# Attention heads told apart by row groups instead of masked copies, with the maximum as a ninth row of the score matmul

## The chip, the cores and the metric

The kernel runs on one core of one Trainium2 chip. The metric is the device time of one execution in microseconds (us), the median of several runs. The core has a matrix engine (TensorE: PE for matmuls, PEld for its weight loads), VectorE (DVE), ScalarE (ACT), GpSimd (POOL) and SyncE (SP), which here issues most DMAs. "Granted clock" is the share of TensorE's full clock that the throttle lets through.

## The reference, cut to what matters

One decoder layer with pre-norm: self attention, cross attention to a context, and a mixture of experts. `x` is 64 batches of 128 tokens with 128 features, the context 64 batches of 77 tokens, all in float32. There are 16 heads of 8 features, so that each head's score matmul contracts over only 8 rows.

```python
def _L0_xattn_ref(query, key, value, mask, Wq, bq, Wk, bk, Wv, bv, Wo, bo):
    q = _split_heads(query @ Wq.T + bq)          # 16 heads of 8
    k = _split_heads(key @ Wk.T + bk)
    v = _split_heads(value @ Wv.T + bv)
    scores = jnp.einsum('bhqd,bhkd->bhqk', q, k) / np.sqrt(D_K)
    scores = jnp.where(mask[:, None, :, :] == 0, -1e9, scores)
    p_attn = jax.nn.softmax(scores, axis=-1)
    attn = jnp.einsum('bhqk,bhkd->bhqd', p_attn, v)
    x = attn.transpose(0, 2, 1, 3).reshape(B, S, D_MODEL)
    return x @ Wo.T + bo

x = x + self_attention(layernorm(x))             # no mask, q scaled by 1/sqrt(128), no bias on q, k, v
x = x + cross_attention(layernorm(x), ctx, mask)
x = x + experts(layernorm(x))                    # router, top 2 of 8, 128 -> 512 -> 128
```

## The kernel before

The 64 batches are held in 16 groups of four (`GB`). Attention is a list of 32 jobs: the 16 groups of self attention, then the 16 of cross attention. A job has four units, one for each batch. Sixteen heads are four groups `c` of four heads (`NG`, `HG`), and group `c` is rows 32c to 32c+31 of the transposed queries and keys. One matmul serves four heads at once: one operand has a masked copy for each head, in which the rows of the three other heads are zero.

- `prologue` prepares a job in five items: `norm` (POOL: xn, L159, and the residual's bias row, L166), `trans` (PE transposes, ACT copies xnT), `query` (pq, L236, to qT on DVE, L239 or L241), `key` (pk, L246, to kT on ACT; then POOL writes four masked copies km, L258, and four of the scaled queries qm, L262) and `value` (pv, L271).
- `maxima` computes a unit's scores with queries as rows (`ps`, L292). In cross attention DVE overwrites masked places (`copy_predicated`, L299). DVE takes the negated maximum over the keys (L304).
- `split` cuts the maxima of two units into three bfloat16 parts on POOL. `turn` transposes them on PE (`pm`, L327), ACT copies them (`mt`), and SP sends them to DRAM (`md`, L331) and back as three rows for each `c` (`mrow`, L335).
- `masked` (L350) starts the transposed score tile `pt` of cross attention with a bias matmul; `scores` (L362) adds keys times masked queries; `exps` adds the three rows of the maximum (L374), and ACT takes the exponential (L380).
- `values` (L394) multiplies the exponentials with the values and with ones, four head groups side by side as column groups. DVE divides (reciprocal, L401). `project` (L414) applies the output weights, DVE adds the residual (L418) and takes the statistics for the next norm; `root` computes the reciprocal roots on POOL by a power and a Newton step (L148 to L153).

The order on PE is written out by hand (`manual_schedule`); the other engines' orders come from a scheduler that follows the dependencies. The main loop goes over steps `s`: unit `s` has its maxima taken, unit `s-4` its exponentials, unit `s-5` its values. A step has two half-steps. In a half-step, two score tiles of the one unit and two transposed ones of the other are interleaved on PE, one in each of the four row groups; then come the values, and then one item of a list `todo` that holds the next job's prologue, the turns and the projections. The pools `ps_s`, `ps_t`, `ps_o` and `ps_m` have two PSUM buffers each. In steady state a job's eight half-steps end with, in order: pm, pv, tp, py, pm, pq, pk, py.

Before the loop, the statistics and roots of all 16 groups are computed, and the first job's prologue runs alone. After the attention come the router and the experts (L478 on), which the change leaves alone.

Of the kernel before, what the change touches and what calls it, by code (L numbers as in the profile page):

```python
# [8 lines left out]
F32 = mybir.dt.float32  # L9
I32 = mybir.dt.int32  # L10
# [6 lines left out]
H = 16  # L17
# [10 lines left out]
def decoder_layer(  # L28
# [33 lines left out]
    def load(src, shape, name, eng=None):  # L62
# [27 lines left out]
    neg_s = const.tile([P, HG, S2], F32, tag="neg_s", name="neg_s")  # L90
    nc.gpsimd.memset(neg_s, NEG)


    blk = const.tile([P, H], F32, tag="blk", name="blk")
    nc.gpsimd.memset(blk, 1.0)
    nc.gpsimd.affine_select(
        out=blk, in_=blk, compare_op=ALU.is_ge, fill=0.0, base=0,
        pattern=[[-DH, H]], channel_multiplier=1,
    )
    nc.gpsimd.affine_select(  # L100
        out=blk, in_=blk, compare_op=ALU.is_ge, fill=0.0, base=DH - 1,
        pattern=[[DH, H]], channel_multiplier=-1,
    )
    hm = const.tile([P, HG], F32, tag="hm", name="hm")
    nc.vector.tensor_reduce(hm, blk.rearrange("p (g j) -> p j g", j=HG), AX.X, ALU.add)

# [7 lines left out]

    vms = []
    for n in range(3):
        t = const.tile([P, GB * NG, HG, 32 + DH], F32, tag=f"vm{n}", name=f"vm{n}")
        nc.gpsimd.memset(t, 0.0)
        vms.append(t)

# [3 lines left out]
    ones_b = const.tile([P, P], BF16, tag="ones_b", name="ones_b")  # L124
    nc.gpsimd.memset(ones_b, 1.0)
# [60 lines left out]

    def attention():
        jobs = [(cross, g) for cross in (False, True) for g in range(NGRP)]
        NB = len(jobs) * GB
        with (  # L190
            tc.tile_pool(name="grp", bufs=2) as grp,
# [6 lines left out]
        ):  # L198
            G = [dict() for _ in jobs]
# [11 lines left out]
            def prologue(n):  # L211
# [6 lines left out]
                def norm():  # L218
                    loads(n + 1)
                    v["xn"] = normalised(g)  # L220
                    add_row(g, bo_s if cross else bff_s)
                    if cross:
                        v["off"] = grp.tile([P, GB, S2], I32, tag="off", name="off")
                        nc.vector.tensor_scalar(v["off"], v["mask"], 0.0, None, ALU.is_equal)
                        v["bias"] = grp.tile([P, GB, S2], BF16, tag="bias", name="bias", bufs=3)
                        nc.gpsimd.tensor_scalar(
                            v["bias"], v["mask"], 0.0, NEG, ALU.is_equal, ALU.mult
                        )
# [4 lines left out]

                def query():
                    pq = ps_m.tile([P, T], F32, tag="mm", name="pq")
                    nc.tensor.matmul(pq, wq_, v["xnT"], start=True, stop=True)  # L236
                    v["qT"] = grp.tile([P, T], F32, tag="qT", name="qT")
                    if cross:
                        nc.vector.tensor_scalar(v["qT"], pq, bq_s, scale, ALU.add, ALU.mult)  # L239
                    else:  # L240
                        nc.vector.tensor_scalar(v["qT"], pq, scale, None, ALU.mult)  # L241

                def key():
                    src = v["ctx"].rearrange("p b k -> p (b k)") if cross else v["xnT"]
                    pk = ps_m.tile([P, GB, K], F32, tag="mm", name="pk")
                    nc.tensor.matmul(  # L246
                        pk.rearrange("p b k -> p (b k)"), wk_, src, start=True, stop=True
                    )
                    v["kT"] = grp.tile([P, GB, K], F32, tag="kT", name="kT", bufs=3)
                    if cross:  # L250
                        nc.scalar.activation(v["kT"], pk, AF.Identity, bias=bk_s)
                    else:
                        nc.scalar.copy(v["kT"], pk)

                    v["km"] = grp.tile([P, GB, HG, K], F32, tag="km", name="km")
                    v["qm"] = grp.tile([P, GB, HG, S], F32, tag="qm", name="qm", bufs=3)
                    for j in range(HG):
                        nc.gpsimd.tensor_scalar(  # L258
                            v["km"][:, :, j, :], v["kT"], hm[:, j : j + 1], None, ALU.mult
                        )  # L260
                    for j in range(HG):
                        nc.gpsimd.tensor_scalar(  # L262
                            v["qm"][:, :, j, :], v["qT"].rearrange("p (b t) -> p b t", t=S),
                            hm[:, j : j + 1], None, ALU.mult,
                        )
# [18 lines left out]

            def maxima(i, c):
                n, b = divmod(i, GB)
                cross = jobs[n][0]
                v = G[n]
                K = S2 if cross else S
                rows = slice(32 * c, 32 * c + 32)  # L290
                ps = ps_s.tile([P, HG, K], F32, tag="s", name="ps")
                nc.tensor.matmul(  # L292
                    ps.rearrange("p j k -> p (j k)"),
                    v["qT"][rows, b * S : (b + 1) * S],
                    v["km"][rows, b].rearrange("p j k -> p (j k)"),
                    start=True, stop=True,
                )
                if cross:
                    nc.vector.copy_predicated(  # L299
                        ps, v["off"][:, b, :].unsqueeze(1).to_broadcast([P, HG, K]), neg_s  # L300
                    )
                if b % 2 == 0 and c == 0:
                    v["m", b // 2] = unit.tile([P, NG, 2, HG], F32, tag="m", name="m", bufs=3)
                nc.vector.tensor_reduce(  # L304
                    v["m", b // 2][:, c, b % 2, :], ps, AX.X, ALU.max, negate=True
                )

            def split(n, p):

                v = G[n]  # L310
                m = v.pop(("m", p)).rearrange("p c b j -> p c (b j)")
                mb = unit.tile([P, NG, 3, 2 * HG], BF16, tag="mb", name="mb", bufs=3)
                r = unit.tile([P, NG, 2 * HG], F32, tag="mr", name="mr", bufs=3)
                nc.gpsimd.tensor_copy(mb[:, :, 0, :], m)
                nc.gpsimd.tensor_tensor(r, m, mb[:, :, 0, :], ALU.subtract)
                nc.gpsimd.tensor_copy(mb[:, :, 1, :], r)
                nc.gpsimd.tensor_tensor(r, r, mb[:, :, 1, :], ALU.subtract)
                nc.gpsimd.tensor_copy(mb[:, :, 2, :], r)
                v["mb", p] = mb

            def turn(n, p):

                v = G[n]
                mb = v.pop(("mb", p))
                R = NG * 3 * 2 * HG
                pm = ps_m.tile([P, P], BF16, tag="mm", name="pm")
                nc.tensor.transpose(pm[:R], mb.rearrange("p c s x -> p (c s x)"), ident_b)  # L327
                mt = unit.tile([P, P], BF16, tag="mt", name="mt", bufs=3)
                nc.scalar.copy(mt[:R], pm[:R])
                md = dram.tile([R, P], BF16, tag="md", name="md")  # L330
                nc.sync.dma_start(md, mt[:R])  # L331
                mrow = unit.tile([P, 2, HG * P], BF16, tag="mrow", name="mrow", bufs=3)
                part = 2 * HG
                for c in range(NG):
                    nc.sync.dma_start(  # L335
                        mrow[32 * c : 32 * c + 3].rearrange("p b x -> p (b x)"),
# [339 lines left out]
```

## Time and profile before

| | |
|---|---|
| median of 3 runs | 2305.23 us (2303.49 to 2306.25) |
| profiled execution, its own time | 2304.34 us |
| its span, first to last instruction | 2302.6 us |
| mean granted TensorE clock | 0.884 |
| PE busy | 1971.4 us, 86% |
| PEld busy | 1250.6 us, 54% |
| DVE busy | 832.6 us, 36% |
| ACT busy | 724.5 us, 31% |
| POOL busy | 769.4 us, 33% |
| first score matmul | at 95.75 us |
| first cross attention scores | at 651.20 us |
| router and experts | from about 1294 us to the end |

How to read the lines that follow: a group of instructions has its line, engine, operation, output and inputs with their shapes and count, then the busy time in us and the mean duration in ns, then the idle time of the engine ahead of it and what ended most of that. A line of the timeline has its start in us, its length in us, engine, line and operation, and in brackets the idle time before it with what released it. A line of the list of waits has the total in us, the number of times and the longest. A row "PE" or "POOL" of digits is the span in 40 slices, in tenths busy, and "PEclk" the granted clock in tenths. A matmul in float32 is recorded as two instructions, each with a weight load.

### The profile page before, as it was taken

The numbers are of one execution on the slowest core, as the hardware profiler recorded it, in microseconds if no ns is written. First come the engines' busy times: TensorE is split into PE (matmuls) and PEld (weight loads), VectorE is DVE, ScalarE is ACT, GpSimd is POOL, SyncE is SP. The second block draws the span as 40 slices with busy tenths as digits, with TensorE's granted clock in tenths as the row PEclk, the third lists the DMA queues.
The fourth block names the chain that finished last, engine by engine and source line by source line (L and its number), as shares of the span: only waits on it lengthen the run. The fifth ranks groups of instructions, "written<-read, shape, count | busy, mean of one in ns | idle before, by whom it ended". The sixth has DMA issues, their size and how long they took to land.

```text
span 2302.6 us, 40698 instructions
## 1 busy us (share of the span) xinstructions
PE 1971.4 (86%) x17475; PEld 1250.6 (54%) x17475; DVE 832.6 (36%) x2045; ACT 724.5 (31%) x1321; POOL 769.4 (33%) x1125
## 2 busy tenths in 40 slices
PE   1297877878778788887878989999999999999999
PEld 0043433434444444444444667777777777777776
DVE  3154544545455556565656221111111111111111
ACT  0032322323222222222222343333333333333333
POOL 5955556456564646464553440000000000000000
PEclk9587878878787878787878769999999999999999
DMA  6000000000000000000000000000000000000000
GB/s 178 0 6 4 5 4 4 5 4 4 4 9 12 12 12 10 15 9 15 9 7 4 2 1 3 4 4 5 5 5 5 6 5 5 5 5 6 5 5 10
DMA packets 39940, 24.25 MB, mean 11 GB/s; under 512 B 17856, under 2 KB 37968, under 8 KB 39760
## 3 DMA queue, kind: packets, MB, share of 16 engines
q1 hardware_dynamic: 36352, 16.59, 2.8%
q0 software_dynamic: 1056, 4.19, 0.6%
q8 instruction: 136, 2.23, 0.4%
q10 hardware_dynamic: 2352, 0.88, 0.2%
q14 instruction: 44, 0.36, 0.1%
HBM read 15.89 MB, written 5.77 MB: 9 GB/s over the span
## 4 chain that ended last, share of the span: by engine, by line
PE 64%; POOL 28%; DVE 3%; issue 3%; DMA 1%; ACT 0%; SPq 0%; ACTq 0%; POOLq 0%; DVEq 0%
PE py L592 20%; PE ph L570 19%; POOL qm L262 9%; POOL km L258 7%; PE ps L292 7%; PE po L394 7%; POOL xn L159 5%; PE pt L362 2%; PE pv L271 2%; POOL xs L166 2%; PE pt L374 2%; POOL rstd L149 1%; PE pt L350 1%; PE tp L173 1%; DVE r L401 1%
## 5 line engine op out<-in xcount | busy, mean ns | idle before, releaser
L574 ACT ACTIVATE hT<-ph,b_s 128x512 f32<-128x512 f32 x512 | 351.6, 687 | 565.3 <-PE ph L570 565.3
L292 PE MATMUL ps<-km,qT 32*128 32x512 f32 (+1 forms) x1024 | 310.8, 675 | 240.5 <-POOL km L258 237.8
L592 PEld LDWEIGHTS py<-w_s,hT 128*128 128x128 f32 x4096 | 477.3, 192 | 55.7 <-issue 53.6
L380 ACT ACTIVATE e<-pt 128x512 f32<-128x512 f32 (+1 forms) x512 | 276.9, 592 | 723.1 <-PE pt L374 712.3
L592 PE MATMUL py<-w_s,hT 128*128 128x128 f32 x4096 | 481.8, 275 | 0.0
L570 PE MATMUL ph<-xT,w_s 128*128 128x512 f32 x1024 | 465.0, 597 | 1.1 <-ACT junk L508 1.1
L304 DVE TENSOR_REDUCE m<-ps 128x4 f32<-128x512 f32 (+1 forms) x512 | 286.7, 579 | 306.1 <-PE pt L362 188.0
L598 DVE SCALAR_TENSOR_TENSOR xs<-py,comb,xs 128x128 f32<-128x128 f32 x512 | 144.1, 344 | 694.5 <-PE py L592 694.5
L362 PE MATMUL pt<-qm,kT 32*128 32x512 f32 (+1 forms) x1024 | 350.6, 754 | 0.0
L570 PEld LDWEIGHTS ph<-xT,w_s 128*128 128x128 f32 x1024 | 186.4, 192 | 187.5 <-issue 186.1
L292 PEld LDWEIGHTS ps<-km,qT 32*128 32x128 f32 x1024 | 99.4, 220 | 345.5 <-POOL km L258 248.1
L159 POOL TENSOR_SCALAR xn<-xs,stat,rstd 128x128 f32<-128x128 f32 x192 | 150.6, 798 | 384.8 <-PE tp L173 384.8
L262 POOL TENSOR_SCALAR qm<-qT,hm 128x512 f32<-128x512 f32 x128 | 202.1, 1594 | 75.2 <-DVE qT L239 42.2
L299 DVE COPY_PREDICATED ps<-off,neg_s 128x308 f32<-128x308 int32 x256 | 127.6, 508 | 229.2 <-PE ps L292 226.9
L394 PEld LDWEIGHTS po<-e,vm 128*32 128x32 f32 (+1 forms) x4096 | 121.4, 123 | 103.2 <-issue 100.1
L394 PEld LDWEIGHTS po<-e,ones_w 128*32 128x32 f32 (+1 forms) x4096 | 116.2, 119 | 97.2 <-issue 95.2
L258 POOL TENSOR_SCALAR km<-kT,hm 128x512 f32<-128x512 f32 (+1 forms) x128 | 165.6, 1315 | 1.1
L394 PE MATMUL po<-e,vm 128*32 128x128 f32 (+1 forms) x4096 | 164.3, 310 | 0.0
L394 PE MATMUL po<-e,ones_w 128*32 128x128 f32 (+1 forms) x4096 | 155.5, 298 | 0.0
L401 DVE RECIPROCAL r<-po 128x256 f32<-128x256 f32 x64 | 112.3, 1755 | 37.3 <-PE po L394 37.2
L374 PE MATMUL pt<-mrow,ones_b 3*128 3x512 bf16 (+1 forms) x512 | 118.0, 430 | 0.0
L350 PE MATMUL pt<-ident_b,bias 128*77 128x512 bf16 x256 | 87.3, 426 | 0.0
(121 smaller groups left out, 1260.1 us busy)
## 6 DMA issues: line engine op xcount, KB each, us to landing
xs<-in_x_dram SPq DMA_DIRECT2D x16, 256.0 KB
w_s<-in_w_dram POOLq DMA_DIRECT2D x2, 2048.0 KB, 17.6
mrow<-md SPq DMA_DIRECT2D x256, 6.0 KB
out_dram<-xs SPq DMA_DIRECT2D x16, 256.0 KB
ctx<-in_ctxT_dram SPq DMA_DIRECT2D x16, 154.0 KB
mask<-in_mask_dram SPq DMA_DIRECT2D x16, 154.0 KB
md<-mt SPq DMA_DIRECT2D x64, 24.0 KB
wq_s<-in_wqT_dram ACTq DMA_DIRECT2D x1, 64.0 KB
```

The costliest lines, as they stand in the source:

```text
L159: nc.gpsimd.tensor_scalar(xn[:, b, :], xs[g][:, b, :], stat[:, i, 0:1], rstd[:, i : i + 1], ALU.subtract, ALU.mult,)
L258: nc.gpsimd.tensor_scalar(v["km"][:, :, j, :], v["kT"], hm[:, j : j + 1], None, ALU.mult)
L262: nc.gpsimd.tensor_scalar(v["qm"][:, :, j, :], v["qT"].rearrange("p (b t) -> p b t", t=S), hm[:, j : j + 1], None, ALU.mult,)
L292: nc.tensor.matmul(ps.rearrange("p j k -> p (j k)"), v["qT"][rows, b * S : (b + 1) * S], v["km"][rows, b].rearrange("p j k -> p (j k)"), s ...
L304: nc.vector.tensor_reduce(v["m", b // 2][:, c, b % 2, :], ps, AX.X, ALU.max, negate=True)
L362: nc.tensor.matmul(v["pt", b, c][:K].rearrange("p j q -> p (j q)"), v["kT"][rows, b, :], v["qm"][rows, b].rearrange("p j q -> p (j q)"), s ...
L374: nc.tensor.matmul(pt[:K].rearrange("p j q -> p (j q)"), ones_b[three, :K], v["mrow", b // 2][three, b % 2, :], start=False, stop=True,)
L380: nc.scalar.activation(e[:K], pt[:K], AF.Exp)
L394: nc.tensor.matmul(po[32 * c : 32 * c + 32, :], w[:, 32 * j : 32 * j + 32], v["e", b, c][:K, j, :], start=(j == 0), stop=(j == HG - 1),)
L570: nc.tensor.matmul(ph, w1_s[:, e, c * P : (c + 1) * P], xT[g], start=True, stop=True)
L574: nc.scalar.activation(hT[:, c, :], ph, AF.Gelu, bias=b1_s[:, i : i + 1])
L592: nc.tensor.matmul(py[:, b, :], hT[:, c, b * S : (b + 1) * S], w2_s[:, e * NFC + c, :], start=(c == 0), stop=(c == NFC - 1),)
```

## The change

Queries and keys get a layout in which each head has its own rows: head r of group c lies in rows 32c to 32c+7, with r along the free dimension (`qh` and `kh`, three of each, rotating over the jobs). `spread` makes it: the projected tile is written to DRAM from ACT's queue and read back by four DMAs on SP's queue, one for each c. A ninth row of `kh` is set to one once; the ninth row of `qh` receives the negated maxima, again by a trip through DRAM. A head's score matmul then contracts over 8 rows, and the transposed one over 9, which adds the maximum without a matmul of its own. The masked copies, the three-way split and the rows of the maximum go; in cross attention the mask's bias is also added to `ps` by a matmul, in place of DVE's overwriting. The scaled queries come from ACT and no longer from DVE. All four score tiles of a half-step are issued by one function.

```diff
-    neg_s = ...                                   # and blk, hm, ones_b
+    bqs_s = const.tile([P, 1], F32, tag="bqs_s", name="bqs_s")
+    nc.scalar.activation(bqs_s, bq_s, AF.Copy, scale=float(DH) ** -0.5)
...
+            qhs, khs = [], []
+            for n in range(3):
+                t = heads.tile([P, HG, GB, S], F32, tag=f"qh{n}", name=f"qh{n}")
+                qhs.append(t)
+                t = heads.tile([P, HG, GB, S], F32, tag=f"kh{n}", name=f"kh{n}")
+                nc.gpsimd.memset(t, 1.0)
+                khs.append(t)
...
-                        v["off"] = grp.tile([P, GB, S2], I32, tag="off", name="off")
-                        nc.vector.tensor_scalar(v["off"], v["mask"], 0.0, None, ALU.is_equal)
...
+                def spread(t, K, heads):
+                    d = dram.tile([P, GB * K], F32, tag=f"d{K}", name="d")
+                    nc.scalar.dma_start(d, t)
+                    src = d.rearrange("(c r d) x -> c d r x", r=HG, d=DH)
+                    for c in range(NG):
+                        nc.sync.dma_start(
+                            heads[32 * c : 32 * c + DH].rearrange("p r b t -> p r (b t)")[
+                                :, :, 0 : GB * K
+                            ],
+                            src[c],
+                        )
+
                 def query():
...
-                        nc.vector.tensor_scalar(v["qT"], pq, scale, None, ALU.mult)
+                        nc.scalar.activation(qT, pq, AF.Copy, scale=scale)
+                    v["qh"] = qhs[n % 3]
+                    spread(qT, S, v["qh"])
...
-                    for j in range(HG):
-                        nc.gpsimd.tensor_scalar(
-                            v["km"][:, :, j, :], v["kT"], hm[:, j : j + 1], None, ALU.mult
-                        )
-                    for j in range(HG):
-                        nc.gpsimd.tensor_scalar(
-                            v["qm"][:, :, j, :], v["qT"].rearrange("p (b t) -> p b t", t=S),
-                            hm[:, j : j + 1], None, ALU.mult,
-                        )
+                    spread(kT, K, khs[n % 3])
...
+                for r in range(HG):
+                    for v, b, rows, pt, still, moving in tiles:
+                        nc.tensor.matmul(
+                            pt[:, r, :], v[still][rows, r, b, :], v[moving][rows, r, b, :],
+                            start="bias" not in v or r == 0, stop="bias" not in v,
+                        )
+                for v, b, rows, pt, still, moving in tiles:
+                    if "bias" in v:
+                        one = (v["bias"][:, b, :], ident_b)
+                        left, right = one if still == "kh" else one[::-1]
+                        K = right.shape[-1]
+                        nc.tensor.matmul(
+                            pt, left, right.unsqueeze(1).to_broadcast([P, HG, K]),
+                            start=False, stop=True,
+                        )
...
-                if cross:
-                    nc.vector.copy_predicated(
-                        ps, v["off"][:, b, :].unsqueeze(1).to_broadcast([P, HG, K]), neg_s
-                    )
...
-            def split(n, p):
...
             def turn(n, p):
...
+                pm = ps_m.tile([P, P], F32, tag="mm", name="pm")
+                nc.tensor.transpose(pm[:R], m, ident)
+                mt = unit.tile([P, P], F32, tag="mt", name="mt", bufs=3)
                 nc.scalar.copy(mt[:R], pm[:R])
+                md = dram.tile([R, P], F32, tag="md", name="md")
+                nc.scalar.dma_start(md, mt[:R])
+                nc.sync.dma_start(
+                    v["qh"][DH::32, :, 2 * p : 2 * p + 2, :].rearrange("p r b q -> p r (b q)"),
+                    md.rearrange("(c r b) q -> c r (b q)", c=NG, b=2),
                 )
...
-                three = slice(32 * c, 32 * c + 3)
-                nc.tensor.matmul(
-                    pt[:K].rearrange("p j q -> p (j q)"),
-                    ones_b[three, :K], v["mrow", b // 2][three, b % 2, :],
-                    start=False, stop=True,
-                )
```

Here `tiles` is the half-step's list of score tiles, two `ps` (queries stationary, keys moving, 8 rows) and two `pt` (keys stationary, queries moving, 9 rows), each in its own row group.

## The prediction

> **What bounds the kernel now.** I read the page first (share of each engine, the 40 slices), then who waited for whom, then the PE timeline of one job, then single weight loads, then the DMA waits.
>
> ```profile
> span 2302.6 us, 40698 instructions
> POOL 5955556456564646464553440000000000000000
> PEclk9587878878787878787878769999999999999999
> L262 POOL TENSOR_SCALAR qm<-qT,hm 128x512 f32<-128x512 f32 x128 | 202.1, 1594 | 75.2 <-DVE qT L239 42.2
> L258 POOL TENSOR_SCALAR km<-kT,hm 128x512 f32<-128x512 f32 (+1 forms) x128 | 165.6, 1315 | 1.1
> ```
>
> POOL works in the attention only (slices 1 to 22 of 40), at about half its time, and there TensorE is granted 0.7 to 0.8 of its clock, not the 0.98 to 1.00 that the table by stage gives for the expert part (1360 to 2302 us). Half of POOL's work is qm and km: 367.7 of 769.4 us. An average of 50% doesn't make a bound; the list of waits does:
>
> ```profile
> PE ps L292 <- POOL km L258: 237.8, 31, 37.3
> ```
>
> TensorE waits 31 times for the last masked copy of the keys, once per job (32 jobs: 16 self, 16 cross, each eight half-steps). The PE timeline of one self job:
>
> ```profile
> 318.54 1.12 PE L246 MATMUL pk<-xnT,wk_s 128*128 128x512 f32 x2
> 319.60 0.69 PE L292 MATMUL ps<-km,qT 32*128 32x512 f32 x1
> ...
> 320.56 0.39 PE L374 MATMUL pt<-mrow,ones_b 3*128 3x512 bf16 x2
> 320.88 1.08 PE L394 MATMUL po<-e,ones_w 128*32 128x128 f32 x32
> 321.89 0.71 PE L414 MATMUL py<-wff_s,aT 128*128 128x128 f32 x4
> 330.16 1.22 PE L292 MATMUL ps<-km,qT 32*128 32x512 f32 x1 [7.55 <-POOL km L258]
> ```
>
> Read it by starts: scores 0.96 us (319.60 to 320.56), maximum rows 0.32, values 1.01, then one extra item. After the projection of the keys PE has one half-step, about 3 us, and then stands for 7.55 us, since qm and km are eight POOL instructions of 1.57 us. After the wait the same score instruction takes 1.22 us and not 0.69: the clock has fallen. The two half-steps that follow take 4.58 and 4.27 us (294.87 job) where 2.5 and 3.4 would do: 3.0 us. It depends on the length of the wait:
>
> ```profile
> 155.73 0.69 PE L292 MATMUL ps<-km,qT 32*128 32x512 f32 x1 [2.40 <-POOL km L258]
> 686.09 0.88 PE L292 MATMUL ps<-km,qT 32*128 32x308 f32 x1 [4.82 <-POOL km L258]
> 95.75 2.08 PE L292 MATMUL ps<-km,qT 32*128 32x512 f32 x4 [37.25 <-POOL km L258]
> ```
>
> 2.40 us of waiting left the clock up, 4.82 us did not (0.88 where 0.52 is usual for 308 columns). The third line is the start: POOL's square roots for all 16 groups stand ahead of the first qm and km. From these lines a self job takes (651.20-155.73)/14 = 35.4 us, a cross job (1233.74-651.20)/15 = 38.8.
>
> **The change, part by part.**
>
> *Masks and split gone.* POOL loses 368 us and the three-way split (five small groups, 78 us). The wait of 7.55 (cross 6.50) and its cold half-steps go; so does the 0.4 to 0.8 us that the turn's transpose waits for mb. What is late next is the trip through DRAM, below.
>
> *Scores.* A half-step's four tiles (four row groups) now take 16 f32 matmuls of 128 columns, 32 records each with a weight load, where it was 8 records of 512. The columns streamed are the same. What is new is loads: 32 and not 8. This is the term that matters, so the row first:
>
> ```profile
> 704.48 0.18 PEld L292 LDWEIGHTS ps<-km,qT 32*128 32x128 f32 x1 [0.40 <-issue]
> 704.49 0.14 PEld L362 LDWEIGHTS pt<-qm,kT 32*77 32x77 f32 x1
> 704.49 0.18 PEld L292 LDWEIGHTS ps<-km,qT 32*128 32x128 f32 x1
> 704.50 0.21 PEld L362 LDWEIGHTS pt<-qm,kT 32*77 32x77 f32 x3
> 704.59 0.20 PEld L292 LDWEIGHTS ps<-km,qT 32*128 32x128 f32 x2
> L592 PE MATMUL py<-w_s,hT 128*128 128x128 f32 x4096 | 481.8, 275 | 0.0
> ```
>
> Loads for different row groups start within 20 ns; the second load of a group of 128 columns starts about 0.1 us after its first. So a group can be loaded every 0.1 us and four groups side by side. L592 has this shape on the full array: 481.8/4096 = 118 ns per load-and-matmul pair, its load hidden. And the values stage already issues 32 pairs in 1.01 us over four column groups. I take 8 rounds of 0.122 = 0.98, with 0.07 for the first load 1.05 us, against 0.96. [...] Bounds: 0.95 and 3.4.
>
> *Maximum rows* (L374) gone: 0.32 us per half-step.
>
> *Cross bias.* Copy_predicated (127.6 us of DVE, never what PE waited for in a cross half-step) gives way to two more bf16 bias matmuls of 308 columns, and all four come after the scores. L350's pair takes 0.55 to 0.58 us with the drain; 308/512 of 0.43 adds 0.26: 0.84.
>
> *Half-steps.* Self: 1.05 + 1.01 = 2.06 plus extras (pm 0.15 twice, tp 0.6, py 0.65 twice, pq, pk and pv 1.05 to 1.09: 5.4 per job). But both score tiles are reduced by DVE at 683 ns each before PE may fill them again: 1.05 + 0.13 + 1.37 = 2.55 us at least, 2.8 in the two half-steps behind py, where DVE first does the residual and statistics (0.42 + 0.86). Sum of the eight: 2.8, 3.1, 2.6, 2.65, 2.8, 3.05, 3.05, 2.65 = 22.7 us. The reciprocal (1755 ns) lies beside pv and pq. Cross: (1.05 + 0.84 + 1.01 - 0.07, since two of the four tiles load 77 columns) x 8 + 5.1 = 27.7; DVE needs only 0.95 per half-step.
>
> *The trip.* Behind pk: ACT copies kT (0.59; 0.52 cross), its queue issues the write to DRAM, SP waits for that and issues four reads at 0.26 each; PE's next job needs the first two. The same for q comes one half-step earlier, so keys are last.
>
> ```profile
> SPq L335 <- DMA md<-mt: 83.4, 64, 3.2
> 3.96 0.49 DVE L139 BATCH_NORM_STATS2 st<-xs 128x6 f32<-128x128 f32 x2 [3.96 <-DMA xs<-in_x_dram]
> ```
>
> The nearest rows: 24 KB to DRAM, 83.4/64 = 1.30 plus 0.31 of issue = 1.6 us; 256 KB into SBUF with other loads in flight, issued at 0.80, used at 3.96: 3.2 us. I take the middle, 2.4 us, for the write of 256 KB and for the reads of 64 KB. [...] Keys land 0.65 + 0.1 + 2.4 + 0.3 + 2.4 = 5.85 us after pk; PE has 2.65 us of its own: a wait of 3.2 (bounds: rows' ends, 1.6 to 4.8). That is between 2.40 (warm) and 4.82 (cold): half the cold cost, 1.5. Cross: 154 KB, 5.3 minus 3.5 = 1.8, warm.
>
> *On other queues.* ACT gets 32 query copies (0.59), and 128 DMA issues (md and d) at 0.3 to 0.45, some 65 us in all at 31% busy: hidden between the exponentials, which need 1.2 us of a 2.6 us half-step; each issue waits for ACT's own copy just ahead of it, and what queues behind are exponentials; late by more than 0.2 us they would hold PE's next score tiles. SP has 320 reads and writes for heads and maxima as before; each first read waits for its write to land (2.4 us). Its mask loads wait for POOL's bias, but stand behind the keys' reads in the compiled order; behind them is the md read, with over a step to spare. DVE loses 26 us of qT and off, POOL gains three fills of 1.8 us: both count at the start only.
>
> *Start.* In the new compiled order the first reads of q stand on SP behind a fifth mask load, which waits for POOL's third bias, after all square roots: 6 + roots 32 + twelve xn 9.6 + adds 3.8 + bias 3.8 + fills 12 = 67, plus issues and landing 5: scores begin at 72 and not 95.75. 23 us (10 to 30; POOL's 25.0 us wait for the first mask goes).
>
> *Sum,* against the profiled execution (2304.3 us, span 2302.6; the median is 0.9 above): self 14 x (35.4 - 27.4) = 112; cross 15 x (38.8 - 29.5) = 140; start 23; jobs 0 and 1 3; the last job, without cold half-steps, 5. Together 283: 2021, by the median 2022 us. Router and experts stay.
>
> **Rivals.**
>
> 1. *The DMA wait takes the place of POOL's.* No row shows 64 KB going into eight partitions, and write, wake and read are in series. With keys landing 8 us after pk: self 22.7 + 5.35 + 3.0 = 31.0, cross 27.7 + 4.5 + 2 = 34.2; gain 61 + 70 + 31 = 162: 2143 us; at 11 us some 2246. For it: PE goes cold again. Against: the 1.6 us row. Chance 0.12.
>
> 2. *Weight loads become the bound* (slower). If 32 loads queue at 0.105 (77 columns: 0.07): self half-steps 3.36 + 1.01 + 0.68 = 5.05, job 40.4; cross 2.8 + 0.84 + 1.01 + 0.64, job 42.3. Then 14 x 5.0 + 15 x 3.5 + 13 (tail, job 1) - 23 = +113: 2418 us. It decides from about 85 ns per load, a score stage of 2.7 us. For it: four times the loads, at every half-step. Against: starts 20 ns apart. Chance 0.09; other mishaps of that sign 0.04.
>
> 3. *The trip hides fully* (landing under 3 us): 22.7 and 27.7, gain 178 + 167 + 31 = 376: 1929 us. Chance 0.06.
>
> That the change doesn't do what it says is excluded by the compiled order: qm, km, mrow are gone.
>
> **How the numbers follow.** The forecast has 0.69, its own range 1955 to 2095 (trip at the rows' ends, score stage up to 1.3 us, start). The range reaches into rivals 1 and 3: 1945 to 2190. Faster by over 0.2% (about what a measurement here can tell from no change): forecast and rivals 1 and 3, 0.87, less 0.02 for a trip so long that it eats the gain, 0.85; same 0.02; slower 0.13.
>
> **What would show it.** Right: ps and pt together about 1.05 us per warm half-step, PE's wait at a job's start 1 to 5 us and released by a DMA of kh, no POOL wait, clock 0.9 and over in the attention, first scores near 72 us. Wrong: PEld the busiest row and score stages over 2 us (rival 2); waits for kh over 5 us with doubled score durations behind them (rival 1); ACT or DVE named behind ps and pt for over 0.5 us per half-step.

## The result and the profile after

The changed kernel takes 2458.2 us, median of four runs (2449.9 to 2472.5), against 2304.4 us for the kernel before on the same chip. The ratio is 1.071, with a 95% interval from 1.061 to 1.081: slower, where 2022 us was forecast.

The page of the profiled execution (its own time 2462.1 us):

```profile
span 2460.3 us, 51742 instructions
...
PE 2276.4 (93%) x23363; PEld 1654.2 (67%) x23363; DVE 705.4 (29%) x1740; ACT 755.5 (31%) x1354; POOL 322.0 (13%) x547
...
PE   1688988898899999999999997999999999999999
...
POOL 8212211211221111211111025000000000000000
PEclk8578677857865555556555557999999999999999
...
L303 PE MATMUL ps<-kh,qh 8*128 8x128 f32 (+1 forms) x4096 | 458.3, 375 | 126.3 <-DMA kh<-d 108.4
```

POOL has done what the change asked of it: 322 us and not 769, and no wait of PE names it in the attention. PE is the bound: 93% of the span. But read the rows PE and PEclk one above the other. In slices 13 to 23, the cross attention, PE is at 9 and the granted clock at 5. PE works without a pause at half speed. The table by stage says it in numbers (columns: stretch in us, its length, busy us and count of PE, PEld, DVE, ACT and POOL, granted clock, share of the DMA engines, GB/s):

```profile
750.00:850.00 100.00, 100.00 (x1119) 67.91 (x1113) 29.16 (x66) 22.51 (x41) 15.44 (x24) 0.50 0.10 23
```

In the kernel before, the same stretch has PE busy for 79.7 us at a clock of 0.80:

```profile
750.00:850.00 100.00, 79.69 (x907) 42.12 (x907) 55.10 (x126) 24.62 (x49) 56.26 (x75) 0.80 0.05 11
```

The list of waits has one for the keys, and fewer times than there are jobs. A small one beside it belongs to it ("issue" is time in which the engine waited for nothing that the profile shows):

```profile
PE ps L303 <- DMA kh<-d: 108.4, 17, 36.8
...
PE ps L303 <- issue: 12.5, 4, 4.1
...
SPq L232 <- DMA d<-kT: 131.9, 31, 6.3
```

The longest, 36.8 us, is the start. Of the other sixteen for kh, the timeline has thirteen of 4.6 to 6.4 us, each ahead of a job's first scores: eleven in the self attention and two in the cross attention. Three of the four under "issue" stand at the same place of three more cross jobs, where the keys' reads have just been issued (at 704.26 us for the first):

```profile
706.73 0.46 PE L303 MATMUL ps<-kh,qh 8*128 8x77 f32 x1 [4.09 <-issue]
1157.62 0.46 PE L303 MATMUL ps<-kh,qh 8*128 8x77 f32 x1 [4.02 <-issue]
1259.61 0.46 PE L303 MATMUL ps<-kh,qh 8*128 8x77 f32 x1 [3.92 <-issue]
```

The jobs between these three have no stop: at half clock their own work is so slow that the keys arrive in time. A job that is cold throughout takes 51.5 us. The timeline of one self job shows a wait:

```profile
412.63 1.13 PE L253 MATMUL pk<-xnT,wk_s 128*128 128x512 f32 x2
413.32 1.32 SPq L232 DMA_DIRECT2D qh<-d  x4
413.68 0.37 PE L303 MATMUL ps<-kh,qh 8*128 8x128 f32 x1
...
413.79 0.58 ACT L258 COPY kT<-pk 128x512 f32<-128x512 f32 x1 [0.96 <-PE pk L253]
...
414.40 0.34 ACTq L229 DMA_DIRECT2D d<-kT  x1
...
414.79 1.08 PE L363 MATMUL po<-e,ones_w 128*32 128x128 f32 x32
...
419.30 1.30 SPq L232 DMA_DIRECT2D kh<-d  x4
422.50 0.55 PE L303 MATMUL ps<-kh,qh 8*128 8x128 f32 x1 [5.99 <-DMA kh<-d]
```

The score stage runs from 413.68 to 414.79: 1.11 us for its 32 loads and 32 matmuls. The keys' write is issued at 414.40, and SP, which waits for it to land, issues the reads at 419.30: 4.9 us. The first reads have landed by 422.50: 3.2 us. PE has stood for 5.99 us, and its first score matmul afterwards takes 0.55 and not 0.37 us.

Where the 157.7 us between the two spans lie (times from the first score matmul, ACT's copies of the cross keys and the first router matmul of both traces):

| stage | before | after | difference | forecast |
|---|---|---|---|---|
| start to the first scores | 95.75 | 80.86 | -14.9 | -23 |
| from there to the first cross keys | 546.8 | 547.0 | +0.3 | -115 |
| 15 cross jobs | 15 x 38.8 | 15 x 48.6 | +146.7 | -140 |
| from the last cross keys to the router | 74.0 | 104.4 | +30.4 | -5 |
| router and experts | 1003.6 | 998.8 | -4.8 | 0 |

The self attention gained nothing, the cross attention lost 10 us a job.

### The profile page after: what moved, and what is told of

Its sections match the earlier page's. It is cut to its first block, busy times and chain, and to the rows that moved or that the text cites. A ratio compares the mean times of both kernels' runs of the same rounds, so it can differ in the third digit from the quotient of the medians.

```text
span 2460.3 us, 51742 instructions
## 1 busy us (share of the span) xinstructions
PE 2276.4 (93%) x23363; PEld 1654.2 (67%) x23363; DVE 705.4 (29%) x1740; ACT 755.5 (31%) x1354; POOL 322.0 (13%) x547
## 4 chain that ended last, share of the span: by engine, by line
PE 90%; DMA 5%; POOL 2%; DVE 1%; issue 1%; ACT 0%; SPq 0%; DVEq 0%; ACTq 0%
PE py L556 19%; PE ph L534 18%; PE ps L303 16%; PE po L363 16%; PE pt L312 4%; PE ps L312 3%; PE pv L267 2%; DMA d<-kT 2%; PE pt L303 2%; DMA kh<-d 2%; PE py L383 2%; PE pq L241 2%; PE pk L253 2%; PE tp L149 1%; DMA xs<-in_x_dram 1%; PE pp L467 1%
## 5 line engine op out<-in xcount | busy, mean ns | idle before, releaser
L303 PE MATMUL ps<-kh,qh 8*128 8x128 f32 (+1 forms) x4096 | 458.3, 375 | 126.3 <-DMA kh<-d 108.4
L303 PEld LDWEIGHTS ps<-kh,qh 8*128 8x128 f32 x4096 | 397.8, 273 | 234.7 <-issue 141.2
L303 PE MATMUL pt<-qh,kh 9*128 9x128 f32 (+1 forms) x4096 | 455.2, 375 | 0.0
L303 PEld LDWEIGHTS pt<-qh,kh 9*128 9x128 f32 (+1 forms) x4096 | 374.5, 234 | 2.6 <-issue 2.6
L363 PE MATMUL po<-e,vm 128*32 128x128 f32 (+1 forms) x4096 | 209.5, 370 | 0.0
L363 PE MATMUL po<-e,ones_w 128*32 128x128 f32 (+1 forms) x4096 | 205.8, 365 | 0.0
L312 PE MATMUL pt<-ident_b,bias 128*77 128x512 bf16 x256 | 152.7, 604 | 0.0
L312 PE MATMUL ps<-bias,ident_b 128*128 128x308 bf16 x256 | 107.9, 427 | 0.0
L149 PE MATMUL tp<-ident,xn 128*128 128x128 f32 x192 | 45.5, 379 | 38.7 <-POOL xn L135 38.7
L312 PEld LDWEIGHTS <-bias 128*77 128x77 bf16 x256 | 42.8, 170 | 33.3 <-issue 31.6
```

Source lines behind the costliest of these rows:

```text
L149: nc.tensor.transpose(tp[:, b, :], src[:, b, :], ident)
L303: nc.tensor.matmul(pt[:, r, :], v[still][rows, r, b, :], v[moving][rows, r, b, :], start="bias" not in v or r == 0, stop="bias" not in v,)
L312: nc.tensor.matmul(pt, left, right.unsqueeze(1).to_broadcast([P, HG, K]), start=False, stop=True,)
L363: nc.tensor.matmul(po[32 * c : 32 * c + 32, :], w[:, 32 * j : 32 * j + 32], v["e", b, c][:K, j, :], start=(j == 0), stop=(j == HG - 1),)
```

## The experiments

Three theories were set against each other. Theory 1: the clock is granted by the rows of the array that work, and score matmuls on 8 or 9 rows of each group of 32 are too few. Theory 2: it is the many small matmuls and loads. Theory 3: it is the wait for the keys alone.

### More rows, all zero (`rows32`)

```diff
-                        rows = slice(32 * x, 32 * x + DH)
+                        rows = slice(32 * x, 32 * x + 31)
...
-                        rows = slice(32 * y, 32 * y + DH + 1)
+                        rows = slice(32 * y, 32 * y + 32)
...
-                    v["qh"][DH::32, ...]          # where the maxima land
+                    v["qh"][31::32, ...]
```

`qh` is zeroed once, and `kh` is one in row 31 alone until the keys are read in.

> The changed kernel with zero rows added: the row of minus the maximum moves from row 8 to row 31 of each row group, rows 8 to 30 of the queries are zero, so that a score matmul contracts over 31 or 32 rows per group in place of 8 or 9. The same number of instructions, the same columns, the same result, the same trip. Theory 1 (TensorE's clock is granted by how many rows of the array work, and 34 of 128 are too few): the cross attention is warm, its job falls from 51.5 us to 32 to 34, the clock of 750 to 850 us from 0.50 to over 0.9; sixteen cross jobs give back some 280 us and the self jobs up to 100; the time is 2050 to 2180 us. Theory 2 (what holds the clock down is the 128-column matmuls, two weight loads for each old one): the same columns and loads, so 2440 to 2475 us and 0.50 in the cross attention. Theory 3 (the wait for the keys' trip throws the clock down and nothing else matters): the wait is as long as before, so 2440 to 2475 us.

2196.1 us, ratio to before 0.956 (0.951 to 0.960). The page's clock row:

```profile
PEclk9588898888889888888989699999999999999999
```

The same stage of its table:

```profile
750.00:850.00 100.00, 86.79 (x1463) 61.25 (x1457) 36.03 (x87) 28.06 (x54) 17.12 (x26) 0.85 0.18 36
```

The same instructions over the same columns, with 23 more rows of zeros in each group, take 262 us less. The cross job falls to 36.8 us. Theory 2 is out, and so is theory 3 in its plain form, since here PE waits for keys more often than in the changed kernel:

```profile
PE ps L307 <- DMA kh<-d: 116.2, 31, 25.2
...
PE ps L307 <- issue: 55.6, 16, 4.3
```

The time is a little above the range that theory 1 gave (2050 to 2180 us), the clock of 0.85 below its 0.9 and the job above its 34 us.

### The kernel before on 8 rows (`before_rows8`)

```diff
-                rows = slice(32 * c, 32 * c + 32)
+                rows = slice(32 * c, 32 * c + 8)
```

> The kernel before, where both score matmuls contract over only the first 8 rows of each row group of 32 (it leaves out the scores of three of every four heads, which become those of zero queries); instructions, 512-column shapes, masked copies and waits stay as they are. Theory 1 (too few rows at work): the clock falls where it was near 0.9, and the cross attention, whose values use 77 rows, holds near 0.5; its job rises from 38.8 us to over 48; the time is 2450 us or more. Theory 2 (small matmuls and weight loads): nothing moves, 2290 to 2320 us. Theory 3 (the wait): nothing moves either, 2290 to 2320 us.

2449.5 us, ratio 1.064 (1.059 to 1.070). The page's clock row:

```profile
PEclk9566676776677777776676556999999999999999
```

Its longest wait of PE in the list of waits (us in total, times, longest):

```profile
PE ps L292 <- POOL km L258: 180.1, 30, 37.7
```

With its large 512-column matmuls untouched, the kernel before loses 145 us when its scores work on a quarter of the rows, although its waits for POOL became shorter (180 us in all, 238 before). The time is what theory 1 asked for; its size in one place is not: the cross job rose to 42.0 us, not to over 48, since the clock there was 0.64 to 0.78 and not 0.5. It falls twice in a job here, and the second time with next to no stop: between 841 and 876 us PE waits once, for 0.40 us at 862 us, and the stage from 853 to 862 us is at 1.00, that from 863 to 869 us at 0.50.

### Without the wait (`early`)

```diff
-                if s % GB == 0 and s // GB + 1 < len(jobs):
-                    todo += prologue(s // GB + 1)
+                if (s + 2) % GB == 0 and (s + 2) // GB + 1 < len(jobs):
+                    todo += prologue((s + 2) // GB + 1)
```

(and `todo = prologue(1)` ahead of the loop)

> The changed kernel with the next job's prologue begun two steps (four half-steps) earlier, so that the trip of queries and keys through DRAM ends before the first scores ask for it. Theory 3 (only the wait of 4.6 to 6.4 us per job throws the clock down): no wait, so warm in both attentions; self jobs 23 to 24 us and cross jobs 28 to 30; 1930 to 2000 us. Theory 1 (rows): the waits go, which gives the self attention some 5 us and part of its cold half-steps per job (80 to 200 us over sixteen jobs), but the cross attention has no wait even now and is still near 0.50 and 51 us a job; 2250 to 2380 us. Theory 2 (small matmuls): as theory 1 for this run.

1952.7 us, ratio 0.848 (0.844 to 0.853). Here theory 1, which I favoured, missed by 300 us, and theory 3 hit. Its forecast took the cold cross attention to have no wait, but its long cold stretches begin with the three under "issue". The page's clock row:

```profile
PEclk9579999999999999997569999999999999999999
```

The wait for keys that is left:

```profile
PE ps L303 <- DMA kh<-d: 37.3, 1, 37.3
```

The cross attention's stage:

```profile
750.00:850.00 100.00, 100.00 (x2047) 72.28 (x2043) 51.05 (x127) 38.62 (x75) 28.32 (x46) 1.00 0.17 40
```

PE is as fully busy as in the changed kernel's 750 to 850 us, with the same instructions on 8 and 9 rows, and does 2047 of them where that did 1119: the clock is 1.00 and not 0.50. So few rows do not by themselves throw the clock down in this mix. Only the start's wait is left, and the clock stays up for 770 us (1.00 from 130 to 900 us, with PE busy for 769.89 us of them).

### Both (`rows32_early`)

> Both edits together: zero rows up to 31 or 32 per group, and the prologue two steps earlier. Theory 1: warm throughout the attention and no wait; self jobs of 23 to 24 us and cross jobs of 28 to 29 us, so 1930 to 1990 us, faster than both kernels. Theory 2 (small matmuls): as the earlier prologue alone, within 10 us. Theory 3 (the wait): as the earlier prologue alone, 1930 to 2000 us, and that run would be as fast.

1930.8 us, ratio 0.840 (0.836 to 0.844). The four corners, with the time from the first to the last copy of cross keys over 15 jobs:

| | one wait a job | no wait |
|---|---|---|
| 8 and 9 rows a group | 2458.2 us, cross job 48.6 | 1952.7 us, cross job 27.7 |
| 31 and 32 rows a group | 2196.1 us, cross job 36.8 | 1930.8 us, cross job 27.7 |

The rows are worth 262 us where there are waits and 22 us where there are none. Those 22 us lie at the end: the last cross keys are copied at 858.3 us with 8 and 9 rows and at 857.7 with 31 and 32. Behind the last `ps`, when only the `pt` of two row groups are left, the clock falls in the first kernel, with PE busy throughout, and not yet in the second:

```profile
900.00:920.00 20.00, 20.00 (x257) 13.41 (x255) 3.31 (x7) 5.63 (x11) 2.05 (x6) 0.65 0.01 3
900.00:920.00 20.00, 20.00 (x365) 14.13 (x361) 6.31 (x12) 7.80 (x15) 2.05 (x6) 1.00 0.02 4
```

Neither cause alone makes the loss. That led to theory 4: a stop of PE throws the clock down; score matmuls on 8 and 9 rows can hold a high clock but not win it back, those on 31 and 32 can.

### A single wait (`one_late`, `rows32_one_late`)

If theory 4 is right, one late job among 32 must do lasting harm, and only with few rows.

```diff
+                late = 18
                 if (s + 2) % GB == 0 and (s + 2) // GB + 1 < len(jobs):
-                    todo += prologue((s + 2) // GB + 1)
+                    if (s + 2) // GB + 1 != late:
+                        todo += prologue((s + 2) // GB + 1)
+                if s == (late - 1) * GB:
+                    todo += prologue(late)
```

> The changed kernel with the earlier prologue for every job but one: job 18, the third of the sixteen cross jobs, gets its prologue at the old place, so that its keys come a few us late, once. Theory 4, formed from the last four runs (a stop of PE throws the clock to half; score matmuls on 8 and 9 rows of a group hold a high clock but cannot win it back, those on 31 and 32 rows can): after this one wait the cross attention stays at 0.50 for most or all of the 13 jobs left, at 51 us each in place of 27.7; 2100 to 2260 us. Theory 3 (each wait costs only itself and a short cold stretch): 1953 + 5 + at most 10, so 1955 to 1970 us.

> The same single late prologue, with zero rows up to 31 and 32 per row group. Theory 4 (the rows decide whether the clock comes back): one wait of about 5 us and one or two cold half-steps, then 0.98 to 1.00 again; 1931 + 5 + 5 = 1935 to 1945 us. If the rows had no part in it: as the kernel with 8 and 9 rows and one late prologue.

With 8 and 9 rows, four executions took 1977.9, 1984.1, 2033.8 and 2276.4 us: 25, 31, 81 and 324 us more than without the late job. None lies in either range of the forecast. I give no ratio here: the spread is the finding. Stages of the one execution of the four that was traced, that of 2033.8 us:

```profile
500.00:520.00 20.00, 17.57 (x273) 12.20 (x274) 7.74 (x19) 5.77 (x11) 1.26 (x1) 0.83 0.33 60
520.00:540.00 20.00, 20.00 (x222) 13.16 (x218) 5.69 (x11) 4.83 (x8) 4.42 (x5) 0.50 0.13 30
...
680.00:700.00 20.00, 20.00 (x231) 13.27 (x229) 4.63 (x13) 4.55 (x9) 6.01 (x11) 0.50 0.13 28
700.00:720.00 20.00, 20.00 (x341) 14.47 (x336) 8.60 (x22) 6.27 (x12) 1.26 (x1) 0.80 0.14 36
720.00:740.00 20.00, 20.00 (x397) 14.35 (x395) 10.64 (x24) 7.58 (x15) 6.47 (x11) 1.00 0.23 55
```

Its only waits of PE between 400 and 900 us:

```profile
PE ps L303 <- DMA kh<-d: 2.4, 2, 2.1
```

The wait of 2.1 us ends at 512.7 us. Some 190 us at half clock follow it, with PE busy all the time, and then the clock comes back by itself, with no wait near. With 31 and 32 rows, the four executions lie between 1937.6 and 1946.1 us, median 1941.9, ratio 0.843 (0.841 to 0.846). There the same late job makes a wait of 1.9 us, and the clock is back at 1.00 by the stage from 540 us:

```profile
520.00:540.00 20.00, 20.00 (x335) 13.82 (x333) 7.82 (x17) 6.90 (x13) 6.47 (x11) 0.78 0.14 31
540.00:560.00 20.00, 20.00 (x414) 14.52 (x403) 10.36 (x23) 7.67 (x15) 5.66 (x6) 1.00 0.15 36
```

Theory 4 holds in kind: even the shortest of the four executions on 8 and 9 rows loses more to the late job (25 us) than the longest on 31 and 32 (15 us). Its number for the first kernel (2100 to 2260 us) assumed that the clock would hardly come back. It comes back after a time that differs from one execution to the next, and within one: in the trace of the changed kernel, the five stops of 3.9 to 4.6 us in the cross attention are followed by some 7, 14, 427, 92 and 229 us at 0.50. What sets that time is open.

### The dose (`rows16`, `rows24`)

The edit is that of `rows32`, with rows up to 16 and 24 in each group and one wait a job.

> The changed kernel with its prologue at the old place (one wait a job) and zero rows up to 15 and 16 per row group: the dose between 8 and 9 rows (2458 us) and 31 and 32 (2196 us). Theory 4 (more rows at work, sooner back at full clock): between the two, 2230 to 2430 us, the cross attention's clock between 0.5 and 0.88. If there were one threshold, met only by 32: 2440 to 2475 us; met by 16 already: 2180 to 2215 us.

> The changed kernel with its prologue at the old place (one wait a job) and zero rows up to 23 and 24 per row group, 92 and 96 rows of the array in all: between 16 (2440 us) and 32 (2196 us). Theory 4 with a bound near half of the rows, as 64 rows, in four groups of 16 or two of 32, were too few so far: the clock comes back as with 32, 2180 to 2260 us. If the bound were near all 128 rows: 2400 to 2460 us.

16 rows: 2439.6 us, ratio 1.061 (1.053 to 1.068). 24 rows: 2413.4 us, ratio 1.046 (1.041 to 1.051). The dose is 2458, 2440, 2413 and 2196 us for 8, 16, 24 and 32 rows: nearly all of the gain is in the last step. A bound near half of the array's rows, which I had expected for 24, is wrong for the cross attention. The page's clock row for 24 rows shows the two attentions apart:

```profile
PEclk9588888888955656555555557999999999999999
```

The self attention (slices 3 to 10) is as warm as with 32 rows, the cross attention (slices 12 to 23) as cold as with 8. The score matmuls work on the same rows in both. What differs, among other things, is the values, whose matmuls contract over 128 keys there and 77 here; the next run changes their rows (and holds the exponentials in eight fixed tiles), nothing else.

### More rows in the values alone (`vals128`)

```diff
-                e = unit.tile([P, HG, P], F32, tag="e", name="e")
+                e = es[(i * NG + c) % 8]            # eight fixed tiles
+                if jobs[n][0] and not jobs[n - 1][0] and b < 2:
+                    nc.vector.memset(e[64:], 0.0)
...
-                K = S2 if jobs[n][0] else S         # in values
+                K = P
```

> The changed kernel with its prologue at the old place; in the cross attention the matmuls of values and sums contract over all 128 rows in place of 77, the added rows of the exponentials being zero. Scores stay on 8 and 9 rows; columns and instructions are the same but for eight small memsets. Theory 4 widened (what counts is the rows at work over all of PE's work, not the scores' alone): the cross attention comes back from a wait as the self attention does, its clock rises from 0.50 to 0.65 or more and its job falls from 51.5 to 36 to 46 us; 2220 to 2380 us. If only the scores' rows counted, or the cross attention stays cold for another reason: 2440 to 2475 us.

2254.1 us, ratio to before 0.978 (0.971 to 0.985): 204 us less than the changed kernel, with its scores still on 8 and 9 rows and its waits still there. The page's clock row:

```profile
PEclk9577785866788988888889889999999999999999
```

The cross attention's stage:

```profile
750.00:850.00 100.00, 90.27 (x1534) 64.27 (x1534) 37.34 (x90) 28.96 (x56) 21.96 (x35) 0.85 0.16 32
```

The cross job is 37.3 us at a clock of 0.85. So the rows of the values count too, not those of the scores alone, and rows of zeros count.

### The effect by itself (`warm8`, `warm32`)

```diff
+            for n in range(32):
+                zs = [...]                           # four PSUM tiles, one for each row group
+                for r in range(HG):
+                    for x in range(NG):
+                        rows = slice(32 * x, 32 * x + 8)      # or + 32
+                        nc.tensor.matmul(
+                            zs[x][:, r, :], z[rows, :], z[rows, :], start=True, stop=True
+                        )
             todo = prologue(1)
```

> The disputed effect by itself. The fastest kernel so far (1909 us), and ahead of its first scores, where PE waits for the first keys anyway, 512 extra matmuls of zeros by zeros, four row groups side by side, 128 columns, on 8 rows of each group, in 128 rounds; their results are not used. From a cold start PE is then busy with nothing but 8-row matmuls. Theory 4: the clock stays at 0.50 for all of them, 128 rounds of 0.21 us are 27 us, and the first scores come some 14 us later than without; 1915 to 1930 us. If busy time alone raised the clock: 1.00 within some 7 us, rounds of 0.11 us after that, 18 us in all, and 1895 to 1910 us.

> The same 512 extra matmuls of zeros, on all 32 rows of each row group. Theory 4: PE goes from 0.50 to 1.00 within some 7 us, the rounds fall from 0.21 to 0.11 us, about 18 us in all, and the real scores may begin warm, which took 30 us at half clock so far; 1890 to 1915 us. If rows had no part in it: the same as with 8 rows.

1961.7 us (ratio 0.854, 0.849 to 0.859) and 1932.7 us (0.841, 0.836 to 0.846), 52 and 23 us above the kernel that they are built on, and both above their ranges. My durations were too short: a float32 matmul is two records, 1024 in all and not 512, and a round of four took 0.26 and 0.15 us. They ran from 63.9 to 129.7 us on 8 rows and from 63.1 to 101.7 us on 32. In this place PE had just done the prologue and began them at full clock, so the test became a sharper one. Stages of 5 us on 8 rows a group:

```profile
65.00:70.00 5.00, 4.96 (x98) 4.68 (x96) 0.00 (x0) 0.00 (x0) 4.75 (x12) 0.66 0.30 87
70.00:75.00 5.00, 5.00 (x79) 4.68 (x77) 0.00 (x0) 0.00 (x0) 5.00 (x12) 0.50 0.54 79
120.00:125.00 5.00, 5.00 (x86) 4.79 (x84) 0.00 (x0) 0.00 (x0) 0.00 (x0) 0.50 0.00 0
```

On 32 rows a group:

```profile
65.00:70.00 5.00, 5.00 (x143) 4.51 (x140) 0.00 (x0) 0.00 (x0) 4.75 (x13) 1.00 0.22 50
80.00:85.00 5.00, 5.00 (x136) 4.42 (x130) 0.00 (x0) 0.00 (x0) 4.60 (x14) 1.00 0.01 3
110.00:115.00 5.00, 5.00 (x21) 2.50 (x22) 1.29 (x2) 0.70 (x2) 0.77 (x1) 0.50 0.21 73
```

On 8 rows PE loses the full clock within some 5 us of unbroken work and stays at half for the 55 us that follow. On 32 rows it keeps the full clock: 1.00 in every stage up to 105 us. The last line is the real start of the attention behind it, in which only two of the four row groups have scores: after idle gaps of 0.8 us in all (100 to 105 us) the clock goes to 0.50 again, and stays there with PE busy for all of the 5 us. That is an observation beside the test, since PE also prepares the next job there.

### The kernel before, without its wait (`before_early`)

The edit is that of `early`, in the kernel before.

> The kernel before with its prologue two steps earlier too, nothing else: the masked copies on GpSimd are begun four half-steps sooner, and their wait of 6.5 us a job can go. Theory 4: without the wait its clock stays near 1.00 and TensorE alone sets a job: the self job of the changed kernel without waits (22.8 us) and 8 times the 0.32 us of the maximum's own matmul, 25.4 us, the cross job 24 to 27 us; 1930 to 1990 us, and the change itself would then be worth under 2% either way. A rival: GpSimd, with some 21 us of work a job by its share of 55% of a 38 us job, has too little left of a 25 us job and becomes the bound; 2000 to 2100 us.

2263.3 us, ratio 0.983 (0.980 to 0.985). Neither range holds it: the nearer one, with GpSimd as the bound, ends 163 us below. The list of PE's waits:

```profile
PE pm L327 <- POOL mb L318: 169.2, 58, 6.6
...
PE ps L292 <- POOL km L258: 37.5, 1, 37.5
```

The wait for the masked copies is gone but for the start, and another has taken its place: on POOL the split of the maxima (`mb`) now stands behind eight masked copies of 1.1 to 1.6 us. With this one edit in both, the change is worth 311 us (1952.7 against 2263.3): what it takes off POOL is worth having once nothing stops PE.

### A version faster than both (`rows32_early_pred`)

```diff
+                if jobs[n][0]:
+                    nc.vector.copy_predicated(
+                        ps, v["off"][:, b, :].unsqueeze(1).to_broadcast([P, HG, S2]), neg_s
+                    )
```

with no bias matmul for `ps`.

> The fastest so far (31 and 32 rows, prologue two steps earlier), with the cross attention's S tiles masked by a predicated copy on VectorE again in place of the 308-column bias matmul. TensorE loses 256 matmuls of 308 columns, 0.13 us each at full clock by 308 columns of the 512 that take 0.22, 34 us in all; VectorE gains 256 copies of about 0.5 us, 8 a half-step pair, and goes from 0.50 to some 0.85 of the cross attention. If TensorE stays the bound: 1890 to 1905 us. If VectorE's longer path to the free S tile makes PE wait: 1915 to 1960 us.

1909.4 us, ratio 0.828 (0.826 to 0.831), 21 us below the same kernel with the bias matmul and 4 us above the forecast's end. The cross job falls from 27.7 to 26.6 us where 8 x 0.26 = 2.1 had been expected. DVE's busy share in the cross attention is 0.77, and PE is still busy for all of it at 1.00. Why only half of the matmuls' streaming time comes back was not tried.

## Why the prediction was wrong, point by point

- **The score stage held.** 1.11 us against 1.05; rival 2 needed 2.7. The loads of four row groups do go side by side: 32 of them, with their matmuls, fit into the 1.11 us. No run shows the upper bound of 3.4 us, which is 32 loads one after another at rival 2's 0.105 us.
- **The half-steps held.** Without waits (`early`) a self job takes 22.8 us and a cross job 27.7; the sums had 22.7 and 27.7.
- **POOL held.** No wait of PE names qm, km or mb any more.
- **The start was mis-sized.** First scores at 80.86 us and not at 72. The path was the one forecast: SP's first reads stand behind a mask load that waits for POOL's third bias. That ended at 72.7 us and not at 67, and issues and landing took 8.1 us and not 5.
- **The trip was mis-sized.** The key's write took 4.9 us in the job shown and the reads 3.2, where both had 2.4; the wait was 5.99 us and not 3.2. The eleven self jobs that waited did so for 5.6 us on average, the five cross jobs for 4.3 us and not 1.8. All waits behind the start sum to 84 us (71.6 for kh and 12.5 under "issue"), where 14 x 3.2 and 15 x 1.8 make 72. That these are near each other is luck: fewer jobs waited, each for longer. But the waits themselves explain only 12 us of the miss. Why the write takes 4.9 us was not tried; the four reads of the queries are issued just ahead of it.
- **The failed step is the price of what follows a wait:** "half the cold cost, 1.5" for a self job, and "1.8, warm" for a cross job. Both were read from the kernel before, where a cold stretch ends after two half-steps and a wait of 2.40 us left the clock up. Those figures belong to matmuls on 32 rows of every group. The change takes them to 8 and 9. There a self job with its wait takes 33.5 us (from 319.16, where one wait ends, to 352.70, where the next does): 22.8 of work, 5.3 of waiting and 5.4 of cold price, where 1.5 was forecast. On 31 and 32 rows the same sum (`rows32`, from 200.90 to 232.10 us, a wait of 5.8) leaves a cold price of 2.6, near the 3.0 that the kernel before showed. In the cross attention, three waits of about 4 us were followed by some 427, 92 and 229 us at half clock, where nothing was forecast. That it is the rows is shown by `rows32`, which keeps the waits and gains 262 us, and by `warm8` against `warm32`. The miss in the span, 441 us, is 286 in the cross jobs (15 x (48.6 - 29.5)), 115 in the self attention, 35 in the tail, 8 at the start, less 5 behind it.
- **The sign in rival 1 was missed.** Its wait came, at about its size (5.35 and 4.5 us there, 5.6 and 4.3 measured), with "PE goes cold again". But it priced a cold stretch at 2 to 3 us, as in the kernel before, and so ended at 2143 us. The changed kernel's stage from 750 to 850 us is 100.00 us busy at 0.50. Up to 1050 us PE goes on without a gap (300.00 of 300 us) and the clock stays at 0.50, so busy time alone does not bring it up here.

A hint in the trace of before was there, at its start: from 95 to 124 us only two of four row groups have scores, and the clock stays at 0.50, also from 100 to 110 us, where PE is busy for 10.00 of 10 us. I had put that down to the wait ahead of it. PE has gaps in the rest of that stretch, so it is a hint and no proof.

## What to carry to other kernels

When a change cuts the contraction of small matmuls, count the rows of the array that work in each stage, and take the price of a stop from a stage with as few rows; a price read from fuller matmuls did not carry over here (5.4 us on 8 and 9 rows against 2.6 on 31 and 32, for one self job with its wait). Rows of zeros cost no time here (27.7 us a cross job without waits, with them and without), so pad each row group to 32 rows where the layout allows it, and hide every stop of PE first: here the earlier prologue alone turned +7% into -15%. A stage in which PE is at 100% and the granted clock at 0.50 is not a full engine (1119 matmul records in 100 us here, 2047 at 1.00); look for what holds the clock.

## What the runs showed of the hardware

- In these runs the granted clock depended on the rows at work, not on busy time alone, and zeros counted: 8 of 32 rows in all four groups, zeros, PE busy throughout (`warm8`): from 1.00 to 0.50 in about 5 us, and 0.50 for 55 us more. 32 of 32, zeros too (`warm32`): 1.00 for 38 us.
- In a mix of 8-row scores and 77-row values both clocks last: 1.00 for 770 us (`early`), 0.50 for 190 us (`one_late`) and from 750 to 1100 us (the changed kernel), at 100% busy each time. In the trace of `one_late`, a stop of 2.1 us led from the high one to the low one; in the kernel before on 8 rows (`before_rows8`), the clock fell from 1.00 to 0.50 with no stop longer than 0.40 us near it. The way back came with more rows (`vals128`, values on 128 rows: 0.50 to 0.85 as the mean of 750 to 850 us) or after a time that varied: one late job cost from 25 to 324 us.
- With one wait a job, the step from 24 to 32 rows a group saves 217 us, that from 8 to 24 only 45. Whether a threshold or a weighted mean over a window stands behind that stays open, and so does whether it is rows or the cells of the array that count: every run that added rows added cells with them.
